# A transformer block on one core: the attention's vector and scalar work put in written order, with its sums moved

## The chip, the cores and the metric

The kernel runs on one core of a Trainium2 chip. A core has TensorE (PE, matrix products; PEld is its weight load), VectorE (DVE), ScalarE (ACT), GpSimd (POOL) and SyncE (SP, which issues most of the transfers). The metric is the device time of one execution, in microseconds (us). Three executions of the kernel before took 1391.32, 1385.78 and 1390.47 us; their median is 1390.47.

## The reference: what is computed

A block over T = 2048 tokens of E = 512 elements: a layer norm, then differential attention and a mixture of experts side by side on the normalised tokens, both added to the input.

```python
xn = layernorm(x)
# attention: 16 heads, each with two queries and two keys of 16 elements; interleaved rotary on q and k
a1, a2 = softmax(mask(q1 k1^T) * 16**-0.5), softmax(mask(q2 k2^T) * 16**-0.5)     # causal
attn1, attn2 = concat(a1 v1, a1 v2), concat(a2 v1, a2 v2)
f = (rfft(attn1) - lam * rfft(attn2)) * filt       # over the tokens; lam from four small vectors
attn = rmsnorm(irfft(f)) * (1 - LAMBDA_INIT) @ Wout
# experts: top 2 of 8 by a softmax gate (352 wide), and one shared expert (704 wide)
y = sum_k weight_k * (silu(xn w1) * (xn w3)) w2  +  (silu(xn sw1) * (xn sw3)) sw2
out = x + attn + y
```

The filter along the tokens is linear, so the kernel joins the two softmaxes first (`attn1 - lam * attn2`) and filters once.

## The kernel before, in words

There are three stages. **Before the attention** (to about 255 us) the tokens are normalised and transposed into `xnT`, values go to `vd`, queries and keys are made, turned and written to HBM, the gate's ranks give each token its places in the experts' lists, and the shared expert is done for the first four tiles of 128 tokens. **The attention** (`middle`, about 255 to 1265 us) has everything else of the experts woven into it. **The ending** (`ending`) applies the filter by products with fixed matrices, the norm and the projection, and adds the experts' rows, which it gathers by indirect transfers.

`middle` is what changes. Heads go in 8 pairs g; for each pair there are four turns, qc = 3, 2, 1, 0: 512 queries against all keys up to them. A turn is a `Chunk`. Its work comes in units: a unit is one head's block of 128 keys against up to 512 queries, for both softmaxes (29, 21, 13 and 5 units a turn, 544 in all). For each unit

- `scores` (L741) multiplies on TensorE into `ps_s` (two buffers of two PSUM banks), ScalarE takes the exponential into a place `pt` of the pool `prob` (L765), and where the block is on the diagonal ("masked" below) GpSimd zeroes what lies above it (L770);
- when both heads of a key block are there, `values` (L781) multiplies the places with `vd` into `ps_o` (L796, one bank) and, in the same function, adds the places on VectorE into the turn's `sum` tiles (L804 the first time, a copy; L806 after), two buffers for each head. When a turn's last values are in, ScalarE copies `ps_o` to `o_sb`.
- At a turn's end `sums` (L811) adds `sum` over the keys by 32 small matmuls into `ps_sum` (L818) and VectorE copies that to `s_sb` (L823); `finish` (L825) transposes `o_sb` and `s_sb` (`ps_ot` L830, `ps_st` L831), takes reciprocals, `rcp` (L833, L836), and scales into `o_n` (L838); `put` (L844) adds the two softmaxes' parts into `vd` on GpSimd (L847). When a pair is complete, `folded` (L852) does the first additions of the filter for it, on GpSimd, in seven pieces.

The loop at L940 takes four units a round, 136 rounds. A round issues: the scores of two units; `values` for what the round before made ready; the scores of two more; values of a next turn if there are any; `put` of turns finished in the round before; `finish` of the turn that ended in the round before; steps of `experts` (L584) until their share of the work is reached; `sums` of a turn whose values ended in this round; and, in rounds without masked units, a piece of `folded`.

`experts` is a generator: each `yield` ends a step and gives its estimated cost. First the shared expert for tiles 4 to 14: `hidden` products of 512 tokens (`wh` L233), tanh on ScalarE (L243), two VectorE operations (L244, L250), then `result` (`wy` L270). Then 36 lists of routed tokens, each in three steps: xh (L169), tanh (L176) and a VectorE product (L177); xg and the product `xu` (L184); and the down product of the list before (`xy` L203), its scaling on ScalarE (L212), the transposition of `xu` (`ps_u` L193) with its copies `uT` (L195, L196), and the transposition of the next tokens (`ps_x` L160). All these, and `ps_sum`, `ps_ot` and `ps_st`, share a ring of three PSUM banks (tag `f`).

What sets the order: L561 says that TensorE, GpSimd and SyncE (with its queue of transfers) execute in the order in which the program writes their instructions. VectorE and ScalarE aren't in that list: their order is set when the kernel is built, by a planner that takes the instruction it expects to be ready first. On the chip each queue is fixed. In the ending all four compute engines are in written order.

The constants come in one transfer, `cst` (L297), whose columns also hold two 128x128 blocks `tri`, used once for the ranks. Two buffers `u_last` hold the half-filled last block of the shared expert's hidden layer.

## Time and profile before

| | |
|---|---|
| median of three executions | 1390.47 us |
| the profiled execution's own time | 1385.58 us |
| its span, first to last instruction | 1383.9 us |
| TensorE busy | 1334.2 us, 96% |
| VectorE busy | 1027.9 us, 74% |
| ScalarE busy | 691.0 us, 50% |
| GpSimd busy | 578.2 us, 42% |
| adds of probabilities (L806) | 576, 639.1 us, 1142 ns each |
| exponentials (L765) | 544, 534.1 us, 1026 ns each |
| masks on GpSimd (L770) | 256, 161.7 us, 655 ns each |
| sums copied (L823) | 32, 9.1 us, 285 ns each |

Busy time counts instructions that run; an engine that waits is idle. In a line of the timeline the first two numbers are start and length in us, then come engine, line, operation, output<-inputs, shape and count; the bracket holds the idle time before it and what ended it. In a line of waits: who waited for whom, then total us, times, and the longest.

### The profile page before, as it was taken

To read this page: it belongs to the slowest core of one execution; us is meant where nothing else is said; L and a number is where in the kernel's file an instruction comes from. 1 tells how busy PE (TensorE), PEld (TensorE's weight loads), DVE (VectorE), ACT (ScalarE), POOL (GpSimd) and SP (SyncE) were. 2 spreads that over 40 slices of the span, in tenths; PEclk is the share of its full clock that TensorE was granted. 3 is DMA by queue.
4 is the path that set the end of the run, shared out by engine and by line. 5 is a ranking of instruction groups with operands and counts; after the bars stand their busy time and mean duration, and the time that the engine had idled before them with its cause. 6 is when DMAs were issued, how large, how long until landed. Compare 5 with 4: busy or idle time off the path is not lost.

```text
span 1383.9 us, 20612 instructions
## 1 busy us (share of the span) xinstructions
PE 1334.2 (96%) x7472; PEld 618.9 (45%) x7472; DVE 1027.9 (74%) x1367; ACT 691.0 (50%) x821; POOL 578.2 (42%) x675
## 2 busy tenths in 40 slices
PE   7999999899999999999999999999999999999998
PEld 3444444333443444444445444544454454445543
DVE  7059881477777778778787888987788778877785
ACT  2311110365655566565666666666566656662321
POOL 0001222011301132036965765665579347532774
PEclk9999999999999999999999999999999999999999
DMA  9406662200210122244455655555655565557997
GB/s 374 167 16 186 195 208 69 87 17 18 76 48 32 37 75 70 80 150 139 173 178 162 214 185 178 177 181 183 201 170 198 189 199 180 170 167 246 193 223 165
DMA packets 74641, 206.58 MB, mean 149 GB/s; under 512 B 12013, under 2 KB 12177, under 8 KB 69153
## 3 DMA queue, kind: packets, MB, share of 16 engines
q1 hardware_dynamic: 61840, 177.62, 39.2%
q0 software_dynamic: 11168, 23.17, 8.3%
q10 hardware_dynamic: 1520, 4.36, 0.9%
q8 instruction: 62, 1.02, 0.3%
q14 instruction: 51, 0.41, 0.1%
HBM read 161.26 MB, written 43.85 MB: 148 GB/s over the span
## 4 chain that ended last, share of the span: by engine, by line
PE 65%; POOL 5%; DVE 4%; ACT 3%; DMA 3%; SPq 2%; issue 2%; ACTq 0%; DVEq 0%; POOLq 0%
PE ps_o L796 16%; PE ps_s L752 12%; PE wh L233 8%; PE xy L203 6%; PE xg L169 6%; PE xh L169 5%; PE wy L270 4%; ACT pt L765 3%; POOL pt L770 2%; PE ps_sum L818 2%; SPq L660 2%; DVE sum L806 2%; POOL res L1023 1%; PE po L1167 1%; PE ps_ot L830 1%
## 5 line engine op out<-in xcount | busy, mean ns | idle before, releaser
L806 DVE TENSOR_TENSOR sum<-sum,pt 128x1024 f32<-128x1024 f32 (+3 forms) x576 | 639.1, 1142 | 129.0 <-ACT pt L765 69.1
L765 ACT ACTIVATE pt<-ps_s 128x1024 f32<-128x1024 f32 x544 | 534.1, 1026 | 207.8 <-PE ps_s L752 164.6
L770 POOL TENSOR_SCALAR_AFFINE_SELECT pt<-pt 128x256 f32<-128x256 f32 x256 | 161.7, 655 | 322.8 <-ACT pt L765 322.1
L796 PE MATMUL ps_o<-pt,vd 128*32 128x512 f32 (+3 forms) x2560 | 266.6, 534 | 2.9 <-POOL pt L770 2.9
L752 PE MATMUL ps_s<-qS,kS 64*128 64x512 f32 (+3 forms) x1280 | 213.1, 414 | 17.0 <-ACT pt L765 15.3
L752 PEld LDWEIGHTS ps_s<-qS,kS 64*128 64x128 f32 x1280 | 100.2, 185 | 183.8 <-ACT pt L765 94.1
L233 PE MATMUL wh<-xnT,wu 128*128 128x512 f32 (+1 forms) x352 | 151.6, 579 | 0.0
L796 PEld LDWEIGHTS ps_o<-pt,vd 128*32 128x32 f32 x2560 | 67.0, 109 | 130.5 <-issue 115.2
L472 POOL DMA_INDIRECT who<-pairs,slot x32 | 33.1, 1036 | 208.2 <-DVE pairs L469 105.9
L847 POOL TENSOR_TENSOR vd<-o_n 128x128 f32<-128x128 f32 x62 | 42.5, 706 | 185.7 <-DVE o_n L838 131.2
L519 PE MATMUL ps_x<-xnT,wqk_sb 128*128 128x512 f32 x256 | 110.5, 593 | 0.0
L203 PE MATMUL xy<-wd,uT 128*128 128x512 f32 (+1 forms) x216 | 101.3, 605 | 0.0
L233 PEld LDWEIGHTS wh<-xnT,wu 128*128 128x128 f32 x352 | 65.1, 192 | 72.2 <-issue 54.9
L169 PE MATMUL xg<-wu,xT 128*128 128x352 f32 x288 | 95.6, 476 | 0.0
L169 PE MATMUL xh<-wu,xT 128*128 128x352 f32 x288 | 93.8, 469 | 0.7 <-ACT xT L162 0.7
L519 PEld LDWEIGHTS ps_x<-xnT,wqk_sb 128*128 128x128 f32 x256 | 48.5, 190 | 60.6 <-issue 60.6
L270 PE MATMUL wy<-wd,wu_t 128*128 128x512 f32 x160 | 73.6, 601 | 0.0
L169 PEld LDWEIGHTS xg<-wu,xT 128*128 128x128 f32 x288 | 53.9, 194 | 32.7 <-DVE sum L806 5.1
L212 ACT ACTIVATE y_sb<-xy,wcol 128x512 f32<-128x512 f32 x36 | 24.7, 687 | 85.8 <-PE xy L203 85.8
L169 PEld LDWEIGHTS xh<-wu,xT 128*128 128x128 f32 x288 | 51.9, 190 | 32.1 <-issue 5.8
L1023 POOL DMA_INDIRECT res<-ys,slot x32 | 55.8, 1743 | 21.5 <-DMA res<-ysh 10.4
L536 ACT CAST hi<-turned 128x1024 fp32r<-128x1024 f32 x16 | 16.7, 1045 | 93.8 <-DVE turned L534 83.1
(238 smaller groups left out, 1389.8 us busy)
## 6 DMA issues: line engine op xcount, KB each, us to landing
wu<-in_wex_dram SPq DMA_DIRECT2D x40, 1408.0 KB
wd<-in_wex_dram SPq DMA_DIRECT2D x39, 768.0 KB
kS<-parts_k SPq DMA_DIRECT2D x128, 128.0 KB
qS<-parts_q SPq DMA_DIRECT2D x256, 64.0 KB
ys<-y_sb SPq DMA_DIRECT2D x36, 256.0 KB
parts_q<-hi SPq DMA_DIRECT2D x32, 256.0 KB
parts_k<-hi SPq DMA_DIRECT2D x16, 256.0 KB
parts_k<-turned SPq DMA_DIRECT2D x16, 256.0 KB
```

The costliest lines, as they stand in the source:

```text
L169: nc.tensor.matmul(dst, xT[:, c, :], w[:, o : o + FI], start=(c == 0), stop=(c == NE - 1))
L203: nc.tensor.matmul(y, uT[:m, ic, :], w[:m, ic * E : (ic + 1) * E], start=(n == 0 and ic == 0), stop=(n == len(pairs) - 1 and ic == NF - 1),)
L233: nc.tensor.matmul(dst, w_sb[o // WUP][0][:, o % WUP : o % WUP + P], x[:, c, :], start=(c == 0), stop=(c == NE - 1))
L270: nc.tensor.matmul(y, us[i][:, t * P : (t + 1) * P], w_sb[i // NF][1][:, i % NF * E : (i % NF + 1) * E], start=(i == 0), stop=(i == SCH - 1),)
L519: nc.tensor.matmul(ps[:, i, :], wqk_sb[st, qk][:, i, c, :], xnT[:, c, cols], start=(c == 0), stop=(c == NE - 1),)
L752: nc.tensor.matmul(to, k, queries[2 * g + h, qc][r, off : off + w], start=True, stop=not general)
L765: nc.scalar.activation(pt[:, :, used], ps[:, :, used], AF.Exp, scale=SCALE)
L770: nc.gpsimd.affine_select(out=part, in_=part, pattern=[[0, 2], [1, P]], compare_op=ALU.is_ge, fill=0.0, base=0, channel_multiplier=-1,)
L796: nc.tensor.matmul(self.o[r : r + 32, off:], vd[:, kb, v0 : v0 + 32], pt[:, s, :], start=first, stop=self.ended, skip_group_check=True,)
L806: nc.vector.tensor_add(to, to, pt)
L847: eng.tensor_add(vd[:, self.qc * TQ : (self.qc + 1) * TQ, v0 : v0 + 32], self.o_n[:, :, h, 0, :], self.o_n[:, :, h, 1, :],)
L1023: nc.gpsimd.indirect_dma_start(out=came[k], out_offset=None, in_=ys, in_offset=bass.IndirectOffsetOnAxis(ap=slot[:, step - 2, order[k] : o ...
```

## The change: what it does

- VectorE and ScalarE join the list of engines in written order.
- The adds leave `values` for a function of their own, `added`, one unit at a time. A round issues them in this order: those held back, the first two units' unmasked ones, the finish, then each expert step followed by one of the other unmasked ones, the rest, and the masked ones last. An add is issued in the round of its own scores, not in the next. `sum` tiles are made at a turn's first add; adds are held back until the sums of the turn before last are issued.
- `sums` moves from the end of the round in which a turn's values ended to the next round, behind that round's first values; its copy to `s_sb` goes to ScalarE, with two buffers. `finish` stays in that next round, at its place after the scores.
- `values` goes on until nothing is left. After the loop, the last two turns are summed, finished and put (on VectorE) one after the other, each with an expert step between.
- The pool `prob` has eight places in place of six (the branch taken here).
- To make room: the product of gate and hidden layer is written over its first factor (`xtanh`, `ws`, the latter with six buffers); one `u_last` in place of two; `uT` has two buffers in place of three; `who_sb` lies in the buffers of `x`; `tri` is loaded on its own, by GpSimd's queue, into a buffer of the first stage.
- In the ending, the product into `u_last` comes ahead of the wider one.

```diff
-            u = mp.tile([P, FI], F32, tag="u", name="xu")
-            nc.vector.tensor_mul(u, g, s)
-            return u
+            nc.vector.tensor_mul(s, g, s)
+            return s
...
-        nc.scalar.dma_start(cst, consts)
+        nc.scalar.dma_start(cst, consts[:, :C_TRI])
...
+        tri_sb = l1.tile([P, 2 * P], F32, name="tri_sb")
+        nc.gpsimd.dma_start(tri_sb, consts[:, C_TRI:])
...
-            pools.enter_context(tc.manual_schedule(engines={mybir.EngineType.PE, mybir.EngineType.Pool, SP}))
+            pools.enter_context(
+                tc.manual_schedule(
+                    engines={
+                        mybir.EngineType.PE, mybir.EngineType.DVE, mybir.EngineType.Activation, mybir.EngineType.Pool, SP,
+                    }
+                )
+            )
...
-            kp, qp, pp = pool("k", 2), pool("q", 2), pool("prob", 5 if general else 6)
+            kp, qp, pp = pool("k", 2), pool("q", 2), pool("prob", 6 if general else 8)
...
-                    for h in range(2):
-                        pt, off = self.probs[h, kb]
-                        to = self.sum[h][:, :, off:]
-                        if first:
-                            nc.vector.tensor_copy(to, pt)
-                        else:
-                            nc.vector.tensor_add(to, to, pt)
...
+                def added(self, unit):
+
+                    for h, kb, *_ in unit:
+                        pt, off = self.probs[h, kb]
+                        if h not in self.sum:
+                            self.sum[h] = ap.tile([P, 2, QC], F32, tag=f"sum{h}", name=f"sum{h}")
+                            nc.vector.tensor_copy(self.sum[h], pt)
+                        else:
+                            to = self.sum[h][:, :, off : off + pt.shape[2]]
+                            nc.vector.tensor_add(to, to, pt)
...
-                    self.s_sb = ap.tile([P, P], F32, tag="s_sb", name="s_sb", bufs=1)
-                    nc.vector.tensor_copy(self.s_sb, ps)
+                    self.s_sb = ap.tile([P, P], F32, tag="s_sb", name="s_sb")
+                    nc.scalar.copy(self.s_sb, ps)
...
+            def added(entries):
+
+                for n, c, unit in entries:
+                    if n < summed + 2:
+                        c.added(unit)
+                    else:
+                        held.append((n, c, unit))
 
             for i in range(0, len(stream), 4):
-                found = burst(stream[i : i + 2])
+                units = stream[i : i + 4]
+                found = burst(units[:2])
                 ended = values()
-                found += burst(stream[i + 2 : i + 4])
-                if todo:
-                    values()
+                for c in closing:
+                    c.sums()
+                    summed += 1
+                found += burst(units[2:])
+                while todo:
+                    ended += values()
                 todo += found
                 for c in closed:
                     c.put(nc.gpsimd)
                     if c.qc == 0:
                         ready.append(c.g)
-                closed = closing
-                for c in closing:
+                closed, closing = closing, ended
+                held, before = [], held
+                added(before)
+                added(u for u in units[:2] if not masked(u))
+                later = [u for u in units[2:] if not masked(u)]
+                for c in closed:
                     c.finish()
                 while worked / work_all < (i + 4) / len(stream):
                     took = next(ex, None)
                     if took is None:
                         break
                     worked += took
-                closing = []
-                if ended is not None:
-                    ended.sums()
-                    closing = [ended]
+                    added(later[:1])
+                    later = later[1:]
+                added(later)
+                added(u for u in units if masked(u))
...
-            for c in closing:
-                c.finish()
-                c.put(nc.gpsimd)
+            ended = []
             while todo:
-                chunk = values()
-            next(ex, None)
-            chunk.sums()
-            next(ex, None)
-            chunk.finish()
-            chunk.put(nc.vector)
+                ended += values()
+            for some in (closing, ended):
+                for c in some:
+                    c.sums()
+                next(ex, None)
+                for c in some:
+                    c.finish()
+                    c.put(nc.vector)
...
-            us.append(times(h[P // 2 :, 3 * P :], s[: P // 2, 3 * P :], u_last[0]))
+            g = several((5, 7, 9))
+            times(h[P // 2 :, 3 * P :], s[: P // 2, 3 * P :], u_last)
```

## The prediction

> **What bounds the kernel now.** I read the page first (busy shares), then busy time by stretch, then what TensorE waited for, then the instructions in order of time around its longest wait.
>
> ```profile
> PE 1334.2 (96%) x7472; PEld 618.9 (45%) x7472; DVE 1027.9 (74%) x1367; ACT 691.0 (50%) x821; POOL 578.2 (42%) x675
> ```
>
> Busy time by stretch (us, TensorE busy, its weight loads, VectorE, ScalarE, GpSimd, granted clock, DMA share, GB/s): the attention's first and second part, the ending, and 15 us inside the second.
>
> ```profile
> 255.00:600.00 345.00, 338.71 (x2009) 140.46 (x2009) 256.77 (x292) 202.40 (x225) 64.27 (x101) 0.99 0.16 53
> 600.00:1265.00 665.00, 644.88 (x4453) 314.19 (x4452) 540.02 (x655) 417.74 (x487) 405.82 (x478) 0.99 0.57 181
> 1265.00:1384.00 119.00, 107.59 (x360) 54.91 (x359) 87.43 (x163) 27.30 (x43) 70.56 (x48) 0.99 0.93 209
> 625.00:640.00 15.00, 12.41 (x91) 6.64 (x90) 13.89 (x17) 5.16 (x7) 11.86 (x12) 0.77 0.28 86
> ```
>
> In the attention (255 to 1265 us) TensorE idles 345 - 338.71 = 6.3 us and 665 - 644.88 = 20.1 us, 26.4 us in all. That is the ceiling of what a better order can give, but for one thing: from 625 to 640 us the granted clock is 0.77, which is 0.23 x 15 = 3.45 us of lost clock. What TensorE waited for, 250 to 1275 us (total, times, longest):
>
> ```profile
> PE ps_s L752 <- ACT pt L765: 15.3, 31, 2.2
> PE ps_st L831 <- DVE s_sb L823: 4.6, 3, 2.6
> PE ps_o L796 <- POOL pt L770: 2.9, 3, 1.6
> ```
>
> The longest that a reordering can touch is the second line. All engines there, in order of time:
>
> ```profile
> 628.33 4.79 DVE L806 TENSOR_TENSOR sum<-sum,pt 128x512 f32<-128x512 f32 x3 [0.30 <-POOL pt L770]
> ...
> 628.81 1.22 POOL L578 DMA_INDIRECT xrow<-xd,tok  x1 [0.16 <-issue]
> ...
> 630.06 1.29 POOL L863 TENSOR_TENSOR xnT<-vd 128x512 f32<-128x512 f32 x1
> ...
> 633.04 0.51 DVE L177 SCALAR_TENSOR_TENSOR xtanh<-xtanh,xh 128x352 f32<-128x352 f32 x1
> 633.48 0.28 DVE L823 COPY s_sb<-ps_sum 128x128 f32<-128x128 f32 x1
> ...
> 633.81 0.47 PE L831 MATMUL ps_st<-cst,s_sb 128*128 128x128 f32 x1 [2.59 <-DVE s_sb L823]
> ...
> 634.07 4.90 PE L169 MATMUL xg<-wu,xT 128*128 128x352 f32 x8
> ```
>
> Three adds of 512 take 4.79 us while GpSimd works; behind them on VectorE stand the expert's product and the 0.28 us copy of the sums; TensorE, at the transposition of that copy, idles 2.59 us, and the eight matmuls after it take 4.90 us, where they take 2.53 elsewhere.
>
> **What the Trainium skill says.** "PSUM — Partial Sum Buffer", Engine vs sequencer instructions: the queues of ScalarE, VectorE and GpSimd are strict FIFO; so what stands behind a waiting instruction waits too, as above. "SBUF — State Buffer", SBUF: two separate sides: a VectorE operation with two SBUF inputs and a GpSimd operation that reads SBUF exclude each other for a whole instruction. The trace agrees: adds range from 0.41 to 3.50 us. "TensorE: Matmul & The Clock Gate", Part 1: half clock after about 3.4 us of idleness, full again after about 3.4 us of work. The trace agrees with the halving but shows it after a gap of 2.59 us, which decides here.
>
> **The change, part by part.** The durations are of the profiled execution: span 1383.9, own time 1385.58 us. It is 4.9 below the median of the three runs, 1390.47; I sum against 1385.6 and keep the 4.9 for the range.
>
> *Sums directly behind values.* The 32 matmuls (1.01 us a turn, 32 turns) stay the same number; they move from the end of the round in which the values ended to the middle of the next, and the copy goes from VectorE (285 ns) to ScalarE. ScalarE shows no such copy; 229 ns (its 128x32 root) and 593 (its 128x512 copy) bound it, 0.30 by size. After the sums come two score units (0.66) and four transposes (0.49) before the copy is needed: 1.15 against 0.30 plus a hop. In ScalarE's order the copy stands ahead of the third exponential, which must wait for those scores anyway. The adds of the turn were issued one or two rounds before, so the sums have no late add to wait for. The three waits for `s_sb` (2.59, 0.79, 1.17) go: -2.59 -0.79, and the clock -3.45. The third is in the tail: there, the adds of the last turn now stand behind the product after tanh at about 1253.5 us, 5.8 us of them end at 1259.3, where TensorE comes to the last sums at 1258.9; about half of the 1.17 is given back: -0.6. Sum -7.4. VectorE loses 32 x 0.285 = 9.1 us of work and 16.0 us of waiting, which alone give nothing.
>
> *VectorE and ScalarE in written order, adds apart from values.* No add is added or removed. One wait is ordered anew: the first add of a turn, a copy, needs the sums of the turn before last to have read the buffer; at a pair's end those run in the same round, up to 4.0 us after its start, and behind the copy on VectorE stand the finish and the product. A round has four units: adds of the first two, the finish, then each expert step followed by one add, then masked adds. Walk of an expert round, from the start of its scores: 0.66 scores, 1.85 values, 0.66 scores, 2.5 for xh or xg: 5.7 us. Exponentials end at 1.5 and 2.5 us; adds of full width take 1.23 unhindered. The product of xg is ready at 5.7, ends at 6.2; two adds follow to 8.7, which is 3.0 of the next round; its first two adds end at 5.5, ahead of the next product. So VectorE carries 5.4 us per 5.7 us round and meets each product in time; real rounds last about 1010/136 = 7.4 us. The adds held behind a product cost nothing while this slack is there: no place is needed again before the second round after. If it is gone, a product is late and TensorE stands at the three-bank ring (`f`) or at `ps_u`.
> The finish is the exception: rcp 0.25, 0.27, o_n 0.69, which free `ps_st` and `ps_ot`. At a head pair's end (last turn to next first), I walk the one at 760 us: 5.8 us of adds from 760.9 on (0.69, two of 1.14, two of 0.50, two of 0.91) plus the 2.07 by which the three adds of 512 there run long (4.80 against 3 x 0.91) end at 768.8; two copies of 0.69, then rcp to 770.4, o_n to 771.4. TensorE reaches the third bank after `ps_ot` at 770.05. It waits 0.4 if it takes `ps_st`'s bank, 1.3 if `ps_ot`'s; I take the middle, 0.85, in four of the seven such ends (those under GpSimd's folding): +3.4. Bounds: 0, and 7 x 1.3 = 9.1.
>
> *Eight places for probabilities.* ScalarE waited for values 40 times, 8.5 us in all (0.2 each), for a place; that wait goes. TensorE gets little: at 315, 440, 563, 695 and 818 us, where it idles 0.46 + 0.41 for an exponential, the two exponentials run back to back (1.94 us for two), and one round has four of them. 0 taken; -4 at most, half of the 8.5.
>
> *Values until nothing is left; last puts on VectorE.* Same instructions in the rounds; two adds of 0.25 us move to VectorE beside a 2.5 us expert step: 0.
>
> *Room made.* Products written over their input, one `u_last`, `uT` twice instead of three times, `who_sb` in the row buffers: each is read, in TensorE's order, before the next writer comes; 0. `tri` as its own load on GpSimd's queue: 131 KB less ahead of the second token tile, at most 131 KB / 374 GB/s = 0.35 us; taken -0.2. GpSimd has one more issue of some 0.7 us (that of `gw_sb`: 0.73) before work that isn't wanted until long after. The order of GpSimd and SyncE is otherwise that of before, so the 2.9 us behind GpSimd's masks stay. In the ending a 0.7 us product moves ahead of another: 0, or +0.3.
>
> Sum: 1385.6 - 7.4 + 3.4 - 0.2 = 1381.4.
>
> **Rivals.** *The stall only moves* (about 1388): VectorE already adds directly behind the exponentials in this trace (an add starts at 610.86, the exponential ends at 610.8), so the separation is there before; and the long adds under GpSimd are not touched. If one holds rcp until TensorE idles 2.5 us, the clock falls once as before: 1381.4 + 6.0 = 1387.4. For it: both causes remain; against: finish comes 1.8 us of work later in the round than the sums.
> *Written order makes the finish late at many turn ends* (slower): o_n stands behind masked adds that wait for GpSimd (53.4 us in 86 waits of VectorE). Price of one: 2.6 idle and 3.4 of clock, 6.0 us. From 1378.0 (the sum without bank waits), two make it as slow as before and four pass 1397.4; with four or five, about 1404. Against: VectorE is busy 540 of 665 us, and the walk has each finish 1 to 2 us behind its transposes.
> *More goes* (about 1368): no bank waits (-3.4), GpSimd's 2.9 and half of the 15.3 us behind exponentials too: 1381.4 - 3.4 - 2.9 - 7.6 = 1367.5. For it: eight places decouple exponentials from values; against: ScalarE's pace there is the work itself.
>
> **How the numbers follow.** Forecast 0.42 (own range 1375 to 1387), moved stall 0.23, late finishes 0.20, more 0.15. 0.5% (7 us) is about what a measurement can tell from no change: faster is below 1383.5, slower above 1397.4. Faster: 0.15 + 0.32 of the forecast; same: 0.10 + 0.23; slower: 0.20. The range leaves out the far half of "more" and most of "late finishes": 1367 to 1398, which also takes in the 4.9 us between the median and the profiled execution.
>
> **What would show it.** Right: no wait of `ps_st` for `s_sb`; the copy at about 0.3 us on ScalarE; clock at full between 260 us and the end; TensorE idle in the attention 20 to 24 us; ScalarE's waits for values gone. Wrong: waits of xg, xy, `ps_sum` or `ps_u` for o_n, rcp or the products that together pass 8 us, or a second halved stretch of the clock.

## The result and the profile after

The changed kernel takes 1382.61 us (median of 20 executions, 1380.11 to 1387.87). The kernel before, run beside it 20 times, takes 1387.59 us (1382.80 to 1391.63; the three executions known ahead of the prediction, with a median of 1390.47, are among these twenty). The ratio is 0.9966, with a 95% interval of 0.9955 to 0.9978: faster, by a third of a per cent, which is less than the 0.5% that the prediction held to be tellable from no change. The profiled execution of after took 1382.72 us, its span is 1380.8 us; before, 1385.58 and 1383.9. So the forecast of 1381.4 us was near. The way there was another one, as the trace shows.

Of the kernel after, first the page's line of busy times, then busy time by stretch in two answers (columns as before: TensorE, its weight loads, VectorE, ScalarE, GpSimd, granted clock, DMA share, GB/s).

```profile
PE 1331.9 (96%) x7472; PEld 620.8 (45%) x7472; DVE 1005.4 (73%) x1337; ACT 692.7 (50%) x853; POOL 598.3 (43%) x673
```

```profile
255.00:600.00 345.00, 340.31 (x2051) 141.78 (x2050) 252.25 (x286) 206.91 (x241) 72.21 (x100) 0.99 0.17 55
600.00:1265.00 665.00, 644.60 (x4447) 318.48 (x4448) 526.83 (x648) 415.63 (x506) 415.40 (x476) 0.98 0.57 182
1265.00:1384.00 119.00, 104.20 (x323) 51.28 (x321) 82.61 (x146) 26.64 (x42) 71.38 (x48) 0.95 0.89 196
...
625.00:640.00 15.00, 10.99 (x41) 5.57 (x40) 11.28 (x14) 3.65 (x5) 10.16 (x15) 0.77 0.37 92
675.00:690.00 15.00, 11.08 (x66) 4.67 (x56) 7.11 (x8) 6.67 (x8) 14.33 (x22) 0.89 0.40 144
770.00:785.00 15.00, 11.93 (x64) 4.41 (x62) 11.92 (x14) 7.53 (x9) 13.95 (x16) 0.89 0.55 163
900.00:910.00 10.00, 8.65 (x46) 3.01 (x39) 7.51 (x7) 6.76 (x8) 9.46 (x10) 0.83 0.55 148
...
1270.00:1280.00 10.00, 7.67 (x14) 3.17 (x14) 4.50 (x7) 1.01 (x1) 3.73 (x4) 0.83 1.03 317
```

Read the clock, the third column from the end, before the busy time. (At "half clock" the chip grants TensorE half of its full clock; 1.00 is the full one.) TensorE idles 20.4 us in the second part of the attention, as before (20.1), but there the clock is now 0.98 instead of 0.99, and in the ending 0.95 instead of 0.99. The short stretches show where: 0.77 over 15 us is a halved clock of 6.8 us, 0.83 over 10 us is one of 3.4 us. The kernel before had one such place in the attention after its start, at 633 us. What TensorE waited for, 250 to 1275 us, kernel after:

```profile
PE ps_s L761 <- ACT pt L774: 12.9, 25, 2.2
PE xy L201 <- DVE rcp L842: 4.0, 1, 4.0
PE ps_o L801 <- POOL pt L779: 3.9, 2, 3.0
PE ps_u L191 <- DVE rcp L842: 2.6, 1, 2.6
PE ps_z L1068 <- DVE vd L1114: 2.3, 1, 2.3
```

The waits for `s_sb` (4.6 us) are gone. In their place stand waits for the reciprocal `rcp`, which frees a bank of the ring `f`. The kernel after, all engines at the first of them, in order of time:

```profile
622.43 8.21 DVE L818 TENSOR_TENSOR sum<-sum,pt 128x768 f32<-128x768 f32 x6
...
622.93 1.49 POOL L585 DMA_INDIRECT xrow<-xd,tok  x1 [0.15 <-issue]
...
624.45 1.30 POOL L872 TENSOR_TENSOR xnT<-vd 128x512 f32<-128x512 f32 x1
...
624.67 0.27 ACT L832 COPY s_sb<-ps_sum 128x128 f32<-128x128 f32 x1 [0.29 <-PE ps_sum L827]
...
630.56 1.54 DVE L815 COPY sum<-pt 128x1024 f32<-128x1024 f32 x2
632.03 0.25 DVE L842 RECIPROCAL rcp<-ps_st 128x16 f32<-128x16 f32 x1
...
632.33 5.49 PE L201 MATMUL xy<-wd,uT 128*128 128x512 f32 x6 [4.01 <-DVE rcp L842]
```

The sums are copied at 624.67 us, by ScalarE, in 0.27 us and in time. But VectorE is then still in six masked adds of the round before, which take 8.21 us beside GpSimd's gather and folding; two first copies follow (1.54), and the reciprocal ends at 632.3. TensorE idles 4.01 us, and its next six matmuls of 512 take 5.49 us; at 1255.81 us of this trace six such take 2.85.

**Where the time went.** For each run I take three marks from the trace, the starts of the first `ps_s`, the first xh and the last xy matmul. They cut the span into the start, the first part (shared expert), the second part (routed experts) and the ending. "Halved" is how long the granted clock was at half in the second part; half of that is taken as full-speed time lost, a little too much where TensorE stood waiting anyway. The last column takes it off. Each row is one profiled execution; after ran twice, and its last column differs by 0.5 us. The run with the fold mixed has after's order up to the last xy, and lies 1.5 us under after; so differences of 2 us in that column are little more than spread. TensorE's matmuls of the first part are the same in every row. Of the second they are too, but for six small ones (0.11 us each) of the ending that stand ahead of the last xy in written order and behind it in before (two under the planner): some 0.7 us less gain in after's second part, and some 0.7 us less loss in its ending, than there was.

| run (order of VectorE, places) | start | first part | second part | ending | halved | second part less lost clock |
|---|---|---|---|---|---|---|
| before (planner, 6) | 255.7 | 350.0 | 662.1 | 116.1 | 6.8 | 658.7 |
| after (written, 8) | 254.8 | 345.8 | 661.6 | 118.6 | 20.5 | 651.4 |
| after, again | 255.3 | 346.0 | 662.1 | 118.6 | 20.5 | 651.9 |
| planner, 8 | 254.4 | 345.8 | 661.7 | 116.1 | 17.1 | 653.2 |
| written, 6 | 254.0 | 347.7 | 665.9 | 118.2 | 20.5 | 655.7 |
| sums late | 254.7 | 346.7 | 663.5 | 118.5 | 20.5 | 653.3 |
| folding later | 253.8 | 351.0 | 662.5 | 118.4 | 10.2 | 657.4 |
| finish first | 254.6 | 345.6 | 655.3 | 118.4 | 6.8 | 651.9 |
| planner, 6 | 254.6 | 348.1 | 663.1 | 115.8 | 10.2 | 658.0 |
| ScalarE written alone, 8 | 254.6 | 345.8 | 654.8 | 116.0 | 3.4 | 653.1 |
| fold mixed | 254.1 | 345.1 | 660.1 | 116.4 | 20.5 | 649.9 |
| finish first, fold mixed | 254.1 | 345.6 | 655.1 | 116.3 | 6.8 | 651.7 |
| copy on VectorE | 254.3 | 345.4 | 661.8 | 119.0 | 17.1 | 653.3 |
| both, by the planner | 255.0 | 345.9 | 662.0 | 116.2 | 17.1 | 653.5 |

From before to after, the start gives 0.9 us, the first part 4.2, the second 0.5, and the ending takes back 2.5: 3.1 us of span. In the second part 7.3 us were gained, and 6.8 us lost again to the clock.

### The profile page after: what moved, and what is told of

Same layout as the page of the kernel before. It is cut to its first block, busy times and chain, and to the rows that moved or that the text cites. A ratio compares the mean times of both kernels' runs of the same rounds, so it can differ in the third digit from the quotient of the medians.

```text
span 1380.8 us, 20566 instructions
## 1 busy us (share of the span) xinstructions
PE 1331.9 (96%) x7472; PEld 620.8 (45%) x7472; DVE 1005.4 (73%) x1337; ACT 692.7 (50%) x853; POOL 598.3 (43%) x673
## 4 chain that ended last, share of the span: by engine, by line
PE 67%; DVE 5%; POOL 3%; DMA 3%; issue 2%; SPq 2%; ACT 2%; ACTq 0%; DVEq 0%; POOLq 0%
PE ps_o L801 17%; PE ps_s L761 12%; PE wh L231 8%; PE xy L201 6%; PE xh L168 6%; PE xg L168 6%; PE wy L269 4%; SPq L669 2%; PE ps_sum L827 2%; DVE sum L818 2%; ACT pt L774 1%; PE po L1196 1%; PE ps_ot L839 1%; PE ps_x L159 1%; DMA kS<-parts_k 1%
## 5 line engine op out<-in xcount | busy, mean ns | idle before, releaser
L818 DVE TENSOR_TENSOR sum<-sum,pt 128x1024 f32<-128x1024 f32 (+2 forms) x576 | 623.4, 1131 | 24.2 <-ACT pt L774 10.7
L774 ACT ACTIVATE pt<-ps_s 128x1024 f32<-128x1024 f32 x544 | 528.1, 1027 | 173.5 <-PE ps_s L761 128.1
L779 POOL TENSOR_SCALAR_AFFINE_SELECT pt<-pt 128x256 f32<-128x256 f32 x256 | 174.9, 708 | 340.5 <-ACT pt L774 277.5
L801 PE MATMUL ps_o<-pt,vd 128*32 128x512 f32 (+3 forms) x2560 | 270.7, 542 | 4.0 <-POOL pt L779 3.9
L761 PE MATMUL ps_s<-qS,kS 64*128 64x512 f32 (+3 forms) x1280 | 209.9, 411 | 14.7 <-ACT pt L774 12.9
L856 POOL TENSOR_TENSOR vd<-o_n 128x128 f32<-128x128 f32 x60 | 37.9, 653 | 137.2 <-DVE o_n L847 129.8
L269 PE MATMUL wy<-wd,ws 128*128 128x512 f32 x160 | 73.6, 601 | 0.0
```

The costliest lines, as they stand in the source:

```text
L269: nc.tensor.matmul(y, us[i][:, t * P : (t + 1) * P], w_sb[i // NF][1][:, i % NF * E : (i % NF + 1) * E], start=(i == 0), stop=(i == SCH - 1),)
L761: nc.tensor.matmul(to, k, queries[2 * g + h, qc][r, off : off + w], start=True, stop=not general)
L774: nc.scalar.activation(pt[:, :, used], ps[:, :, used], AF.Exp, scale=SCALE)
L779: nc.gpsimd.affine_select(out=part, in_=part, pattern=[[0, 2], [1, P]], compare_op=ALU.is_ge, fill=0.0, base=0, channel_multiplier=-1,)
L801: nc.tensor.matmul(self.o[r : r + 32, off:], vd[:, kb, v0 : v0 + 32], pt[:, s, :], start=first, stop=self.ended, skip_group_check=True,)
L818: nc.vector.tensor_add(to, to, pt)
```

## The experiments

In every run below, before was timed on the same chip; ratios are to it. Line numbers are those of each run's own kernel; most agree with after's.

**VectorE and ScalarE left to the planner, the rest as after.**

```diff
-                        mybir.EngineType.PE, mybir.EngineType.DVE, mybir.EngineType.Activation, mybir.EngineType.Pool, SP,
+                        mybir.EngineType.PE, mybir.EngineType.Pool, SP,
```

> The changed kernel with VectorE and ScalarE given back to the planner during the attention; all else of the change kept. If the written order carries the gain, the first xh matmul comes at about 605 us as before the change (599.9 with it) and the ratio to before is about 1.000. If the gain comes from the eight places or from the moved sums, the first xh stays within 1 us of 600 and the ratio is 0.995 to 0.998. If the written order is what puts the finish behind the adds, the waits of xy and ps_u for rcp (4.0 and 2.6 us) shrink below 2 us each and the ratio falls to about 0.992.

Measured: 1376.60 us, ratio 0.9931 (0.9909 to 0.9952), faster than the change: the interval ends below that of after, though the two were not timed beside each other. No wait for the reciprocal is left; the ending is 2.5 us shorter than in after. So the written order, as it stands, costs time; what gained is among the rest of the change.

**Six places for probabilities, the rest as after.**

```diff
-            kp, qp, pp = pool("k", 2), pool("q", 2), pool("prob", 6 if general else 8)
+            kp, qp, pp = pool("k", 2), pool("q", 2), pool("prob", 5 if general else 6)
```

> The changed kernel with six places for probabilities in place of eight. If the places carry the gain of the attention's first part, the first xh comes at about 604 us, ScalarE waits for values again (some 8 us in all) and the ratio is about 0.9995. If places do nothing, as the prediction put it, the first xh stays at 600 and the ratio at 0.9966 within 0.001.

Measured: 1386.01 us, ratio 0.9998 (0.9983 to 1.0013): the whole gain of the change is gone. What ScalarE waited for ahead of its exponentials, 250 to 1265 us, in this run:

```profile
ACT pt L774 <- DVE sum L818: 12.6, 14, 2.8
ACT pt L774 <- PE ps_o L801: 10.8, 38, 1.2
```

With eight places these two lines together are 0.2 us. The table gives the price: 1.9 us in the first part, 4.3 in the second. Lost clock is equal in the two profiled executions (20.5 halved), so this difference isn't the clock's. If anything the ratio makes the places look cheap: in 14 of this run's 22 executions the mean clock was 0.992 to 0.994, where after's twenty lay between 0.986 and 0.989.

**The sums at their old place, at the end of the round, the rest as after.**

```diff
-                for c in closing:
-                    c.sums()
-                    summed += 1
                 found += burst(units[2:])
...
                 added(u for u in units if masked(u))
+                for c in closing:
+                    c.sums()
+                    summed += 1
...
-                for c in some:
+                for c in some if some is ended else []:
                     c.sums()
```

> The changed kernel with the sums back at the end of the round in which the values ended; the copy stays on ScalarE and both engines in written order. If the sums' place carries the gain of the first part (a turn's 1.0 us of sums between two score bursts gives ScalarE time), TensorE's wait for exponentials rises from 12.9 to about 15 us and the first xh comes 2 to 3 us later; ratio about 0.998. If the place does nothing, the ratio stays at 0.9966 within 0.001 and ps_st waits for s_sb not at all, since ScalarE has no adds before it.

Measured: 1384.68 us, ratio 0.9976 (0.9961 to 0.9991). The wait of 3.9 us for `rcp` stays, the second (2.2 us) now falls on `ps_sum`; no wait for `s_sb` comes back, with the copy on ScalarE. The sums' place is worth 0.9 us in the first part and 1.9 in the second by the table, little more than the spread of rows in one order; the intervals of the two ratios overlap, so the time alone wouldn't show it either. By what path isn't shown: TensorE's waits for exponentials, expected to rise to about 15 us, fell from 12.9 to 11.9.

**No folding in the rounds that finish a turn with qc of 1 or 0, and two pieces a round elsewhere as soon as one more pair waits, the rest as after.**

```diff
-                for _ in range(0 if any(map(masked, units)) or not shared else 1 if len(ready) < 2 else 2):
+                for _ in range(0 if any(map(masked, units)) or any(c.qc < 2 for c in closed) or not shared else 2 if ready else 1):
```

> The changed kernel with GpSimd's folding kept out of the rounds in which a turn of qc 0 or 1 is finished (it starts two rounds later, two pieces a round when a pair waits). If the long adds beside the folding hold the finish, and the finish holds the PSUM banks, the waits of xy, ps_u and ps_x for rcp and o_n (7.1 us) and the clock's falls at 631 and 775 us (3.4 and 1.7 us of lost work) go: about 1373, ratio 0.990. If the adds alone hold it, folding or not, the waits stay above 4 us and the ratio at 0.9966 within 0.001. The rival cost: two pieces in one round make masks late (3.9 us before, up to 8).

Measured: 1384.98 us, ratio 0.9995 (0.9979 to 1.0011). This run's VectorE in order of time, at the place of the 4 us wait; the six adds are those that took 8.21 us in after:

```profile
626.71 4.28 DVE L818 TENSOR_TENSOR sum<-sum,pt 128x768 f32<-128x768 f32 x6
```

Without GpSimd's folding beside them they take half as long (the gather is still there, at 627.20 us), and every wait for the reciprocal is gone. The folding, however, came later in a heap, and TensorE waited for the masks behind it (waits of this run, 250 to 1275 us):

```profile
PE ps_o L801 <- POOL pt L779: 12.2, 7, 7.3
```

The 7.3 us are one wait: at 684 us the masks (L779) stand on GpSimd behind the last pieces of one pair's folding and the first of the next. So the cause of the long adds is shown, and this cure costs what it brings. Because the edit also doubled the pieces, it doesn't tell what withholding alone would do. Its first part, in which neither kernel folds, is 5.2 us longer than after's, through one wait of 6.9 us for an exponential at its start (2.2 in after) and a longer halved stretch behind it. So that row says nothing of folding there; it shows how far off a single execution can lie.

**The finish ahead of the adds, the rest as after.**

```diff
                 held, before = [], held
+                for c in closed:
+                    c.finish()
                 added(before)
                 added(u for u in units[:2] if not masked(u))
                 later = [u for u in units[2:] if not masked(u)]
-                for c in closed:
-                    c.finish()
```

> The kernel after, with one thing moved: in each round the end of a turn (reciprocals and products, lines of rcp and o_n) stands on VectorE ahead of the adds of probabilities instead of behind the plain ones of the first half. Theory 'the adds that stand ahead of a turn's end hold the ring of banks': TensorE's waits for the reciprocal (4.0 us at 628 us, 2.6 us at 771 us, 0.5 us for o_n) are gone, and so are the stretches of half clock that follow them (6.8 us at 631 us and 3.4 us at 775 us, worth half of that): 1371 to 1378 us, ratio to the kernel before 0.988 to 0.993. Rival 'the wait moves': the reciprocal now waits on VectorE for ScalarE's copies and TensorE's transposes, the adds behind it come later, and the exponentials or the sums wait for them: waits of TensorE in the attention stay near 29 us in all, ratio 0.995 to 0.999.

Measured: 1376.26 us, ratio 0.9886 (0.9855 to 0.9916). Before read 1391.97 us on this chip, with executions from 1382.7 to 1399.8; this makes the ratio of this run and the next three look some 0.3% better than elsewhere, and they are best held against one another and by their traces. This run's engines in order of time, at the place of the 4 us wait:

```profile
622.34 7.62 DVE L818 TENSOR_TENSOR sum<-sum,pt 128x768 f32<-128x768 f32 x6
...
629.89 0.25 DVE L842 RECIPROCAL rcp<-ps_st 128x16 f32<-128x16 f32 x1
...
630.19 2.85 PE L201 MATMUL xy<-wd,uT 128*128 128x512 f32 x6 [1.14 <-DVE rcp L842]
...
631.05 1.54 DVE L815 COPY sum<-pt 128x1024 f32<-128x1024 f32 x2
```

The masked adds are still in front, since they are of the round before; the two copies are now behind. 1.14 us of waiting instead of 4.01, and six matmuls in 2.85 us: no halved clock. The second wait, 2.6 us, is gone. Of the waits for the reciprocal 5.5 us went, but 4.8 us came in for others: xh for its weights' transfer (3.5) and `ps_o` for masks (5.2 against 3.9). So the second part less lost clock is as long as in after, 651.9 against 651.4 us; what was gained is clock, 6.8 us. It was no accident of one execution: the mean clock was 0.992 or 0.993 in all six. The rival had the sum of the waits right, the theory the time.

**Six places under the planner.**

```diff
-                        mybir.EngineType.PE, mybir.EngineType.DVE, mybir.EngineType.Activation, mybir.EngineType.Pool, SP,
+                        mybir.EngineType.PE, mybir.EngineType.Pool, SP,
...
-            kp, qp, pp = pool("k", 2), pool("q", 2), pool("prob", 6 if general else 8)
+            kp, qp, pp = pool("k", 2), pool("q", 2), pool("prob", 5 if general else 6)
```

> The kernel after, with VectorE and ScalarE left to the planner during the attention and six places for probabilities instead of eight. Theory 'places pay only where the adds stand late in a written order': the same time as with the planner and eight places (ratio to the kernel before 0.9931), within 0.0015; ScalarE waits for places about 10 us in all, none longer than 1 us. Rival 'eight places pay in either order': about 4 us slower than that, ratio 0.995 to 0.997, as six places cost 0.32% in the written order.

Measured: 1382.27 us, ratio 0.9922 (0.9891 to 0.9953); the run below it in the table, on the same chip with eight places under a planned VectorE, took 1378.35 us. The ratios can't tell these apart; the parts can: against the planner with eight places, the first part is 2.3 us longer and the second, less lost clock, 4.8. By the parts, places pay in either order, which is the rival's case, though its ratio isn't the one measured. TensorE's waits behind exponentials in this run, 245 to 1275 us, show some of it:

```profile
PE ps_s L761 <- ACT pt L774: 15.5, 32, 2.2
```

These are 12.9 us in 25 waits with eight places, under the planner as in after, and 15.3 in 31 in the kernel before. And with six places the second part, less lost clock, is nearly that of before (658.0 and 658.7 us): with the places taken out, the rest of the change under the planner moves little there. The first part is still 1.9 us shorter than before's.

**ScalarE alone in written order.**

```diff
-                        mybir.EngineType.PE, mybir.EngineType.DVE, mybir.EngineType.Activation, mybir.EngineType.Pool, SP,
+                        mybir.EngineType.PE, mybir.EngineType.Activation, mybir.EngineType.Pool, SP,
```

> The kernel after, with VectorE alone left to the planner during the attention and ScalarE in written order. Theory 'VectorE's order holds what the written order costs': as fast as with both engines left to the planner, ratio to the kernel before 0.992 to 0.9945, and TensorE's waits for the reciprocal (4.0 and 2.6 us) are gone. Rival 'ScalarE's order does it' (tanh and the copies of the experts behind exponentials): ratio 0.9955 to 0.998 and TensorE waits for tanh's product, y_sb or xT over 5 us in all.

Measured: 1378.35 us, ratio 0.9916 (0.9885 to 0.9947). This run's longer waits of TensorE but those for exponentials, 245 to 1275 us:

```profile
PE ps_o L801 <- POOL pt L779: 3.6, 3, 1.7
PE ps_st L840 <- DVE xtanh L176: 3.1, 2, 2.2
PE xh L168 <- DMA wu<-in_wex_dram: 1.9, 1, 1.9
```

No wait for the reciprocal, an ending of 116.0 us: the cost of written order is VectorE's. The planner has a stall of its own at the same place, 2.2 us of `ps_st`, behind a product that waits for tanh.

**The last pair's folding in another order.** The 32 operations of `folded(NG - 1, nc.vector)` are written out so that neighbours don't depend on one another; one value lies in another free slot.

```diff
-            for _ in folded(NG - 1, nc.vector):
-                pass
+            folded_mixed(NG - 1, nc.vector)
```

```python
add(v[:, :4], f[:, :4], f[:, 4:8])
sub(v[:, 10:12], f[:, 10:12], f[:, 14:16])
sub(v[:, 4:8], f[:, :4], f[:, 4:8])
...
```

> The kernel after, with the last pair's folding on VectorE written in another order: the same 32 operations, but neighbours no longer depend on one another. Theory 'the chain of dependent operations makes the ending late': the folding takes 7 to 8 us instead of 9.4 us, TensorE's wait for it (2.3 us at 1270 us) falls to 1 us or less, and the half-clock stretches at 1273 us and 1311 us (3.4 us each, worth half) go or shrink: 1378 to 1381 us, ratio to the kernel before 0.9930 to 0.9955. Rival 'the ending is set by its transfers and its own chain, not by the fold': first ps_z earlier by about 1 us, end unchanged, ratio 0.9960 to 0.9975.

Measured: 1379.51 us, ratio 0.9914 (0.9882 to 0.9945). VectorE in order of time, first in after, where L882 and L900 read what L867 wrote and L901 overwrites what L900 reads; then in this run:

```profile
1264.94 0.23 DVE L867 TENSOR_SCALAR vd<-vd 128x128 f32<-128x128 f32 x1
1265.20 0.29 DVE L882 TENSOR_TENSOR xnT<-vd 128x128 f32<-128x128 f32 x1
...
1267.93 0.23 DVE L867 TENSOR_SCALAR xnT<-xnT 128x128 f32<-128x128 f32 x1
1268.19 0.29 DVE L900 TENSOR_TENSOR xnT<-xnT 128x128 f32<-128x128 f32 x1
1268.52 0.29 DVE L901 TENSOR_TENSOR xnT<-xnT 128x128 f32<-128x128 f32 x1
```

```profile
1264.28 0.22 DVE L921 TENSOR_SCALAR xnT<-xnT 128x128 f32<-128x128 f32 x1
1264.42 0.23 DVE L921 TENSOR_SCALAR vd<-vd 128x128 f32<-128x128 f32 x1
1264.55 0.22 DVE L950 TENSOR_TENSOR vd<-xnT 128x64 f32<-128x64 f32 x1
1264.69 0.29 DVE L951 TENSOR_TENSOR xnT<-xnT 128x128 f32<-128x128 f32 x1
1264.89 0.29 DVE L952 TENSOR_TENSOR vd<-vd 128x128 f32<-128x128 f32 x1
```

Counted from start to start, an operation of 0.22 us is followed after 0.26 us when the next has to wait for it, after 0.13 when it hasn't; one of 0.29 after 0.33 or 0.20. In the kernel before the planner had put independent operations between dependent ones, and the same 32 ran from 1267.30 to 1274.80 us, 7.5 us. The folding takes 6.9 us (1258.70 to 1265.59) instead of 9.4 (1261.62 to 1271.05; 0.8 of these are the shared expert's last product, written ahead of the folding's last operation and waiting for its input). The wait of `ps_z` is gone, one of 1.7 us comes ahead of `ps_r`, and the ending is 116.4 us instead of 118.6. Of the two halved stretches in the ending the first is gone; that at 1311 us in after stays, at 1306 us. That is the theory's case, at 2.2 us.

**Both of these together, after's own copy on VectorE, both by the planner, and after again.** All four ran on one chip.

```diff
-                    nc.scalar.copy(self.s_sb, ps)
+                    nc.vector.tensor_copy(self.s_sb, ps)
```

(the run with the copy; the other two have the diffs above, the third with the planner's list)

> The kernel after itself, unchanged, beside the three others on the same chip, so that they can be held against it: ratio to the kernel before 0.995 to 0.998, and the waits for the reciprocal of 4.0 and 2.6 us at the same two places. If these waits were an accident of one execution, they are elsewhere or under 2 us.

Measured: 1383.86 us (1380.10 to 1387.35), ratio 0.9965 (0.9953 to 0.9978). The waits of 4.00 and 2.56 us are at the same two places, at 633 and 774.6 us: they belong to the order and not to one execution.

> The kernel after, with both changes of order on VectorE that shortened it one at a time: the end of a turn ahead of the adds, and the last pair's folding with neighbours that do not depend on one another. Theory 'two separate stalls': the gains add, 9 to 11 us under the kernel after on the same chip (ratio of the two 0.992 to 0.9935), no wait for the reciprocal over 1.2 us, and ps_z waits for the folding under 1 us. Rival 'what the first saves is given back before the ending' (its transfers are still under way): no more than 7 us under the kernel after.

Measured: 1376.23 us (1372.35 to 1382.69), ratio 0.9919 (0.9898 to 0.9940), 7.6 us under after on the same chip: between theory and rival by the median. In the profiled execution (1372.71 us) both stalls are short, and the table has both gains, 6.8 us of clock in the second part and 2.3 in the ending. In this run, some of TensorE's waits, 245 to 1275 us, and busy time by stretch:

```profile
PE ps_o L801 <- POOL pt L779: 5.2, 3, 4.0
PE xh L168 <- DMA wu<-in_wex_dram: 2.8, 1, 2.8
...
PE xy L201 <- DVE rcp L842: 1.2, 1, 1.2
```

```profile
600.00:1265.00 665.00, 644.75 (x4460) 318.89 (x4459) 531.66 (x673) 416.02 (x506) 439.14 (x476) 0.99 0.58 185
1265.00:1384.00 119.00, 95.58 (x308) 47.60 (x306) 75.83 (x120) 25.77 (x40) 69.38 (x48) 0.98 0.83 173
```

The clock reads 0.99 and 0.98 where after has 0.98 and 0.95; what is left is the masks' 4.0 us (one wait, as in the finish-first run) and the weights' transfer. This is the fastest profiled execution together with that of ScalarE written alone (1371.0 and 1371.1 us of span), and beats both kernels.

> The order of the program as in the run with both changes, but VectorE and ScalarE left to the planner in the attention. Theory 'the planner undid both stalls already': as fast as with the planner alone, 3 to 7 us under the kernel after on the same chip, and slower than the written order with both changes by 2 to 6 us. Rival 'the planner follows the order of the program where it is free to': within 1.5 us of the written order with both changes.

Measured: 1378.39 us (1376.08 to 1380.87), ratio 0.9928 (0.9913 to 0.9943). It is the planner with eight places once more, in time and by its parts: the planner doesn't take up the order of the program. Its distance to the written order with both edits, 2.2 us, is inside the intervals.

> The kernel after, with the copy of a turn's sums (s_sb) put back on VectorE, in its written place there: behind the adds of the round before and ahead of this round's. Theory 'the early sums alone removed the wait, the engine of the copy is of no account': within 1.5 us of the kernel after on the same chip and no wait of ps_st for s_sb. Rival 'the copy had to leave VectorE': it stands behind late adds, ps_st waits for s_sb again 2 to 8 us in all, and the time rises by 3 to 8 us.

Measured: 1383.45 us, ratio 0.9968 (0.9955 to 0.9981). This run's longest waits of TensorE, 245 to 1275 us:

```profile
PE ps_s L761 <- ACT pt L774: 12.7, 25, 2.1
PE ps_st L840 <- DVE s_sb L832: 9.9, 5, 5.0
```

The wait for `s_sb` is back, 9.9 us of it, as the rival has it (which named 2 to 8); the time is that of after within 0.4 us, as the theory has it. Both, because not one wait for the reciprocal is left: TensorE stands still at `ps_st` for 5.0 us at 630 us where in after it stands at xy for 4.0. The engine of the copy only chooses at which instruction TensorE waits for the same late adds.

## Why the prediction was right in time and wrong in its steps

- **Sums directly behind values (-7.4): the stall moved.** The waits for `s_sb` did go, and the copy is 0.27 us on ScalarE. But the long masked adds were untouched and held the next thing behind them on VectorE, the reciprocal. This is the rival "the stall only moves"; the run with the copy on VectorE shows it. By the run that undoes it, the sums' place is worth 0.9 + 1.9 us.
- **The clock (-3.45, and full from 260 us on): wrong in sign.** Over the whole span it was at half for 17.0 us before and 35.8 after, up to 8.5 us of work lost before and 17.9 after. I counted the clock once, for the wait that I removed, and not for those that I priced. The sign that I had named for "wrong", a second halved stretch, came true: there are five stretches in the second part. The order with the finish first takes most of it back.
- **The finish reaching the ring late (+3.4, 0.85 at four of seven ends): mis-sized.** It was 4.01 and 2.56 us at two ends, and 0.52 behind the second: 7.1 us. I walked the end at 760 us, with adds that run 2.07 us long; at 622 us six take 8.21 us where they take 4.28 without the folding.
- **Eight places (0, at most -4): the step that failed most.** They give 1.9 us in the first part and 4.3 in the second in written order, 2.3 and 4.8 under the planner. I saw that the exponentials of a round run back to back and took ScalarE's pace for the limit. ScalarE's waits for places did go, to 0.2 us; but TensorE's waits for them fell from 15.5 to 12.9 us under the planner, and the rest of the gain is spread over steps that no line of waits names. In written order there is no gain without this part: ratio 0.9998.
- **The ceiling (26.4 us of idle time): no ceiling.** TensorE's idle time in the attention fell only to 4.7 + 20.4 = 25.1 us, not to the 20 to 24 that I had named. What fell is its busy time: the same 2051 matmuls of the first part, between the marks, cover 343.4 us before, 342.1 with six places in written order and 340.5 after, with the same lost clock. So the busy time of the same matmuls held delays that a better order can win back; I priced waits alone.
- **First part and start (-0.2 in all): 4.2 and 0.9 us.** Of the 4.2, places are 1.9 and the sums' place 0.9; 1.4 stays open, and the other parts of the change (values until nothing is left, fewer buffers) were not run alone. The start differs by up to 1.5 us between runs that have it in common, so its 0.9 can't be put down to `tri`.
- **The ending (0, or +0.3): +2.5.** I read the product that moves; what counted was the last pair's folding on VectorE, which the planner had interleaved (7.5 us) and the written order doesn't (9.4). Mixed by hand, the ending is back at 116.4 us.
- **GpSimd's masks (2.9 unchanged):** 3.9 us, one of them 3.0, and the clock halved behind it.
- **The slower rival, late finishes at many turn ends:** there were two, not four. The price of one, taken as 6.0 us, was up to 7.4 at the first (4.0 of waiting, 3.4 of clock) and up to 4.3 at the second (2.6 and 1.7).

So the time came out by luck, because errors cancelled. Laid out by stretch, the forecast was -0.2 us for start and first part, -0.6 for the second part's work, -3.45 for its clock and 0 for the ending: -4.2. Measured were -5.1, -7.3, +6.8 and +2.5: -3.1.

## What to carry to other kernels

When a stall is caused by late work on an engine that keeps its order, moving what waits behind that work to another engine can move the stall to the next instruction in the queue, as here; ask what stands behind the late work, and put the short operation that frees a buffer ahead of it. Price a stall of TensorE with the clock that it can cost as well, and look at the granted clock by stretch before looking at waits. Don't take idle time for all that a better order can give. When a planner's order is written out by hand, go through the chains that it had interleaved, down to the last one.

## What the runs showed of the hardware

**The clock halves behind short pauses.** TensorE in order of time, kernel after:

```profile
902.86 0.50 PE L761 MATMUL ps_s<-qS,kS 64*128 64x512 f32 x2 [0.93 <-ACT pt L774]
903.78 0.50 PE L761 MATMUL ps_s<-qS,kS 64*128 64x512 f32 x2 [0.41 <-ACT pt L774]
904.21 3.25 PE L801 MATMUL ps_o<-pt,vd 128*32 128x512 f32 x16
```

The sixteen matmuls take 3.25 us, 1.92 elsewhere: half clock from 904.7 us on, behind pauses of 0.93 and 0.41 us. Every stretch here but the last is 3.41 us or a multiple of it. The Trainium skill ("TensorE: Matmul & The Clock Gate", Part 1) has windows of about 3.4 us that run freely, so that the result varies between runs of one kernel. The trace agrees with the length and the variation, and with windows that run freely: in after the halved stretches start at 631.59, 682.79 and 774.95 us, 15 and then 27 times 3.413 us apart. It doesn't agree with the whole idle window that the skill asks for: here 1.3 us in two pauses were enough, while in the run with the finish first a wait of 3.48 us (from 786.4 us on, for an expert's weights) left the clock full. In these runs, what a single wait costs can't be told from its length.

**So one kernel's time follows its clock.** The kernel with both edits took 1372.35 us in an execution with a mean clock of 0.995 and 1382.69 with 0.989. After lay between 0.986 and 0.989 in all 16 executions of its second run, before between 0.989 and 0.996 in the 24 beside them. With six places in written order, 14 executions at 0.992 to 0.994 took 1383.1 to 1386.3 us, and 8 at 0.985 to 0.989 took 1387.5 to 1394.9. The planner's run and that with ScalarE alone in written order have nearly the same waits, and second parts of 661.7 and 654.8 us: 6.9 us apart, of which 6.8 are lost clock.

**VectorE overlaps neighbours that don't depend on one another.** The skill ("VectorE: DVE Perf Modes", The DRAIN you can't avoid) says that the next operation doesn't start until the pipe is empty, that one which isn't held starts earlier, and that in a chain of eight copies a semaphore after each cost nothing extra. The trace agrees with the earlier start: an independent operation starts 0.20 us behind the start of one of 0.29 us, so before that one's end, and a dependent one 0.33 us behind it. On the cost of waiting it differs, and the measurement decides: in after, fourteen of the 32 small operations start some 0.12 us later than independent ones would, which makes the 1.7 us by which the folding got shorter, the 0.8 apart.
